# Normalised tokens made feature-major by VectorE and DRAM, with the norm weights in the matrices

## The chip, the cores and the metric

The kernel runs on one core of a Trainium2 chip. Five engines work beside each other: TensorE (PE; its weight loads are listed apart as PEld), VectorE (DVE), ScalarE (ACT), GpSimd (POOL) and SyncE (SP, which here only issues DMAs). The metric is the time of one execution in microseconds on the device. Three executions of the kernel before gave 1006.23, 1006.74 and 1008.61 us; their median, 1006.74 us, is the time before.

## What is computed

Sixteen elements of 256 tokens with 256 features, each with a context of 77 tokens, go through a decoder layer (self attention, cross attention, a gated MLP, each behind an RMS norm), and then through a second block of cross attention, a narrow MLP and self attention with layer norms. Everything is in 32-bit floats. The part that the change touches:

```python
def rmsnorm(x, w, eps=EPS):
    var = jnp.mean(jnp.square(x), axis=-1, keepdims=True)
    return x * jax.lax.rsqrt(var + eps) * w
...
h = rmsnorm(hidden_states, sa_norm_w)
h = residual + attention(h, h, sa_wq, sa_wk, sa_wv, sa_wo)
hn = rmsnorm(h, ca_norm_w)
h = residual + attention(hn, context, ca_wq, ca_wk, ca_wv, ca_wo)
hn = rmsnorm(h, mlp_norm_w)
h = residual + silu(hn @ w_gate) * (hn @ w_up) @ w_down
```

Attention has 16 heads of 16 features. `rmsnorm`'s result is used only as the left side of products with `sa_wq`, `sa_wk`, `sa_wv`, `ca_wq`, `w_gate` and `w_up`.

## The kernel before

Tokens lie on partitions: an element `b` is a tile of 128 partitions x 2 token tiles x 256 features (`h`), loaded by pairs of elements. A product needs its inputs with features on partitions, so that each norm is followed by a transposition.

For each element and each of the three norms (`sa`, `ca`, `mlp`), `rmsnorm` (lines 339 to 354) runs two squares with a sum on ScalarE (L347), a scale on VectorE and a power on GpSimd (`rsqrt`, L195 and L197), and two scalings on ScalarE that write `hn` (L353). `weighted_T` (lines 356 to 366) then transposes `hn` by four 128x128 TensorE transposes (`transposed`, L205) into a PSUM bank, and two ScalarE activations (L365) bring it to SBUF as `hnT`, each with the norm's weights as a scale for each partition. `project_T` (L423) multiplies `hnT` with a matrix: `psq` and `psk` in `self_operands`, `pscq` in `cross_queries`; `psv` (L672) takes `hnT` as the stationary side. In `mlp`, `pg` and `pu` (L752) are gate and up, `wd` (L782) is down. There is one buffer for each of `hnT_sa`, `hnT_ca` and `hnT_mlp`, and three for `hn`.

Attention: `sc` (L498) makes self scores, from which VectorE takes maxima (`nmax`, L503); `st` (L559) makes them again, transposed and with the maxima in, for the exponentials on ScalarE (`pT`, L567); `po` (L601) multiplies with the values. `csc`, `cst` and `cpo` are the same for the cross attention. All of `sc`, `st`, `csc` and `cst` write one tile of four PSUM banks (`ps_sc`), of which there is one. `wo` and `cwo` (L640) are the output projections; VectorE adds them to `h` (L645). Some 32x32 block transposes on VectorE turn attention outputs (L611, L631).

The order of the work is made by a planner written in the kernel (`Order`): each stage of each element is a stream of steps with engines, durations, needs, and buffers that it takes and gives back. The planner keeps a clock for each engine and at each turn takes the step with the best rank among those that can start, where `RANKS` gives each kind of stage a rank. A step of TensorE has a tile shape, full, row or column (`f`, `r`, `c`), with a price for a turn between shapes. `lag` is a time after a step's end until what it gives is there. Instructions are then issued engine by engine in that order, which the engines follow.

SP issues the loads of tokens and contexts, most constants, and the stores of the output. ScalarE issues four matrix loads at the start, GpSimd one. Eight completion counters are shared in turn by the DMAs of SP and ScalarE, so that a DMA's issue waits until the DMA that had its counter eight DMAs earlier has landed.

Of the kernel before, what the change touches and what calls it, by code (L numbers as in the profile page):

```python
# [15 lines left out]
P = 128  # L16
D = 256
# [12 lines left out]
def kernel(  # L30
# [24 lines left out]
    pool = ctx.enter_context(tc.tile_pool(name="work", bufs=2))  # L55
    small = ctx.enter_context(tc.tile_pool(name="small", bufs=2))
    ps_sc = ctx.enter_context(tc.tile_pool(name="ps_sc", bufs=1, space=PSUM))
    ps_po = ctx.enter_context(tc.tile_pool(name="ps_po", bufs=1, space=PSUM))
# [18 lines left out]
    def tokens(ap, u):  # L77
# [3 lines left out]
    BUFS = {  # L81
        "h": 4, "cx": 1, "cx2": 2, "hn": 3, "hnT_sa": 1, "hnT_ca": 1, "hnT_mlp": 1, "ctxT": 1,
        "qx": 3, "kx": 3, "vone": 3, "cqT": 1, "cqx": 1, "ckm": 1, "ckx": 1, "cvone": 2, "pT": 3,
# [25 lines left out]

    def load_matrix(src, name, eng):  # L110
        rows, cols = src.shape
        t = const.tile([P, rows // P, cols], F32, tag=name, name=name)
        eng.dma_start(t, src.rearrange("(c p) n -> p c n", p=P))
        return t

    def load_columns(src, name, eng):
        t = const.tile([P, NC], F32, tag=name, name=name)
        eng.dma_start(t, src.rearrange("(c p) -> p c", p=P))
        return t
# [11 lines left out]
    make_identity(nc, ident)  # L131
    sa_nw = load_columns(sa_norm_w, "sa_nw", nc.gpsimd)

    vones, cvones, maxes = [], [], ([], [])
    for i in range(3):
        t = const.tile([P, QT, NH, 2 * HD], F32, tag=f"vone{i}", name=f"vone{i}")
        nc.vector.memset(t, 1.0)
        vones.append(t)
    wq = load_matrix(sa_wq, "wq", nc.scalar)
    wk = load_matrix(sa_wk, "wk", nc.scalar)  # L140
    wv = load_matrix(sa_wv, "wv", nc.scalar)
    wo = load_matrix(sa_wo, "wo", nc.scalar)
    load_tokens(1)
    ca_nw = load_columns(ca_norm_w, "ca_nw", nc.sync)
    cwk = load_matrix(ca_wk, "cwk", nc.sync)
    cwv = load_matrix(ca_wv, "cwv", nc.sync)
    cwq = load_matrix(ca_wq, "cwq", nc.sync)
    cwo = load_matrix(ca_wo, "cwo", nc.sync)
    mlp_nw = load_columns(mlp_norm_w, "mlp_nw", nc.sync)
    wg = load_matrix(w_gate, "wg", nc.sync)  # L150
    wu = load_matrix(w_up, "wu", nc.sync)
    wd = load_matrix(w_down, "wd", nc.sync)
# [67 lines left out]

    STANDS_BACK = {"rf": 2, "cf": 2, "fc": 10}

# [16 lines left out]
    class Order:  # L239
# [35 lines left out]
        def put(self, st, t):  # L275
# [27 lines left out]
            for k in s.rel:  # L303
                self.freed[k[0]][self.held.pop(k)] = done
            for k in s.gives:
# [6 lines left out]
        def run(self):  # L312
            while self.streams:
                best = None
                aux = []
                for st in self.streams:
                    t = self.start(st)
                    if t is None:
                        continue
                    if st.step.pe:  # L320
                        turn, wait = self.shape + st.step.shape, t - self.clock["P"]
                        late = wait > 100
                        rank = st.rank[0] + STANDS_BACK.get(turn, 0) + 0.05 * wait
                        key = (late, t if late else 0, rank, st.rank[1])
                        if best is None or key < best[0]:
                            best = (key, st, t)
                    else:
                        e = st.step.ops[0][0]
                        aux.append((max(t + T_NEXT, self.clock[e]), st.rank, st, t))
                if aux:  # L330
                    b, _, st, t = min(aux, key=lambda a: a[:2])
                    if best is None or b + sum(o[1] for o in st.step.ops) <= best[2] + best[1].step.pe + 800:
                        self.put(st, t)
                        continue
                assert best, [(st.rank, vars(st.step)) for st in self.streams]
                self.put(best[1], best[2])


    def rmsnorm(b, kind, needs):
# [12 lines left out]
        for t in range(QT):  # L352
            nc.scalar.activation(hn[:, t, :], h[:, t, :], AF.Copy, scale=r[:, t : t + 1])  # L353
        return hn

    def weighted_T(hn, b, w, kind):

        yield Step(
            4 * T_TR, ops=[("A", 470)] * NC, acq=[(f"hnT_{kind}", b)],
            rel=[("hn", f"{kind}{b}")], gives=[(f"hnT_{kind}", b)],  # L360
        )
        tp = transposed(hn, f"{kind}{b}")
        dst = pool.tile([P, NC, S], F32, tag=f"hnT_{kind}", name=f"hnT_{kind}{b}", bufs=1)
        for c in range(NC):
            nc.scalar.activation(dst[:, c], tp[:, c], AF.Copy, scale=w[:, c : c + 1])  # L365
        return dst

# [45 lines left out]

    def project_T(w, srcT, name, steps=None):

        n = srcT.shape[-1]
        for m in range(NC):
            if steps:
                yield next(steps)
            if m == 0:  # L420
                ps = mm_bank(name)
            for c in range(NC):
                nc.tensor.matmul(  # L423
                    ps[:, m * n : (m + 1) * n], lhsT=w[:, c, m * P : (m + 1) * P],
                    rhs=srcT[:, c, :], start=(c == 0), stop=(c == NC - 1),
                )
        return ps[:, : NC * n].rearrange("p (m n) -> p m n", m=NC)
# [219 lines left out]
    def self_operands(a):  # L647
        b = a.b
        hn = yield from rmsnorm(b, "sa", [("x", b // UB)])
        hnT = yield from weighted_T(hn, b, sa_nw, "sa")  # L650
        ps = yield from project_T(wq, hnT, f"psq{b}", in_halves(
            ops=[("A", 690)] * 2, needs=["wq"], acq=[("qx", b)], gives=[a.key("q")]
        ))
        a.qx = a.tile("qx", [P, NC, 2, S])
        masked(a.qx[:, :, 0], a.qx[:, :, 1], ps)
        ps = yield from project_T(wk, hnT, f"psk{b}", in_halves(
            ops=[("V", 545)] * 4, needs=["wk"], acq=[("kx", b)], gives=[a.key("k")],
# [9 lines left out]
        for t in range(QT):  # L667
# [3 lines left out]
            for c in range(NC):  # L671
                nc.tensor.matmul(  # L672
                    ps[:, t * D : (t + 1) * D], lhsT=hnT[:, c, t * P : (t + 1) * P],
                    rhs=wv[:, c, :], start=(c == 0), stop=(c == NC - 1),
# [4 lines left out]
    def cross_keys(pair):  # L679
# [6 lines left out]
        for c in range(NC):  # L686
            for i in range(UB):
# [7 lines left out]
                   acq=[("ckm", u), ("ckx", u)], gives=[t.key("k") for t in pair])  # L695
        ps = yield from project_T(cwk, ctxT, f"psck{u}")
        km = a.tile("km", [P, NC, 2, UB * SK])
# [18 lines left out]
    def cross_queries(a):  # L716
        b = a.b
        hn = yield from rmsnorm(b, "ca", [("h", b)])
        hnT = yield from weighted_T(hn, b, ca_nw, "ca")
        ps = yield from project_T(cwq, hnT, f"pscq{b}", in_halves(  # L720
            ops=[("A", 585), ("A", 690), ("A", 690)], needs=["cwq"],
            acq=[("cqT", b), ("cqx", b)], rel=[("hnT_ca", b)], gives=[a.key("q")],
# [8 lines left out]
    def mlp(b):  # L731
        hn = yield from rmsnorm(b, "mlp", [("ch", b)])
        hnT = yield from weighted_T(hn, b, mlp_nw, "mlp")
        for f in range(0, NF, 2):
            banks = []
            for w, n in ((wg, "pg"), (wu, "pu")):
                if n == "pg":
                    steps = in_halves(
                        ops=[("A", 600), ("V", 690, 1)], needs=["wg"],
                        acq=[("sg", b, f)] + [("gT", b)] * (f == 0), free=f > 0,  # L740
# [6 lines left out]
                for i in range(2):  # L747
# [3 lines left out]
                    for c in range(NC):  # L751
                        nc.tensor.matmul(  # L752
                            ps[:, i * S : (i + 1) * S],
                            lhsT=w[:, c, (f + i) * P : (f + i + 1) * P], rhs=hnT[:, c, :],
                            start=(c == 0), stop=(c == NC - 1),
# [363 lines left out]
    def loads():  # L1119
        for u in range(NU):  # L1120
            yield Step(ops=[("S", 100)], acq=[("h", u)], gives=[("x", u)] * (u > 1), lag=5000)
            if u > 1:
                load_tokens(u)

    def context_loads():
        for u in range(NU):
# [6 lines left out]
    def second_loads():  # L1133
# [5 lines left out]
    order.done.update({  # L1139
        ("x", 0): 5e3, ("x", 1): 20e3, "wq": 8e3, "wk": 9e3, "wv": 10e3, "cwk": 12e3,  # L1140
        "cwv": 13e3, "cwq": 14e3, "wg": 18e3, "wu": 21e3, "wd": 24e3, "late": 14e3, "small": 28e3,
    })
# [4 lines left out]
        "second_constants": (1, 50, 0),  # L1147
        "outputs": (4.5, -1, 50),
        "exponentials": (-2.5, -50, 4),
        "projection": (1.5, -50, 1.5),  # L1150
        "cross_outputs": (3, 0, 50.25),
        "cross_exponentials": (-100, 0, 0),
        "cross_projection": (-50, 0, 0),
        "self_maxima": (0, -50, -100),
        "cross_maxima": (-49, 0, 0),
        "cross_queries": (0, 1, -49.5),
        "self_operands": (-1.5, 0, -0.5),
        "cross_keys": (2, 0, 0),
        "mlp": (4.75, -0.25, -3.5),
        "second_context": (6, 0, -50),  # L1160
        "second": (3, 0, -50),
# [6 lines left out]

    add("loads", 0, 0, loads())
    add("loads", 0, 1, context_loads())  # L1170
    add("loads", 0, 2, second_loads())
# [17 lines left out]
    for u in range(NU):  # L1189
# [6 lines left out]
        mybir.EngineType.PE, mybir.EngineType.Activation, mybir.EngineType.DVE,  # L1196
        mybir.EngineType.Pool,
    }
# [33 lines left out]
```

## Time and profile before

One profiled execution took 1005.27 us, of which the span from its first to its last instruction is 1003.3 us.

| | us | share of span |
|---|---|---|
| profiled execution | 1005.27 | |
| its span | 1003.3 | |
| TensorE busy | 965.4 | 96% |
| VectorE busy | 589.6 | 59% |
| ScalarE busy | 504.4 | 50% |
| GpSimd busy | 81.4 | 8% |
| data moved by DMA | 17.57 MB | |

How to read it. The page lists busy time by engine; divides the span in 40 equal slices with a digit for each engine (tenths of the slice that it was busy; 9 is 90% or more), and for the TensorE clock that was granted; names the chain of work that ended last; and groups instructions by source line, tile, shape and count, with busy time, mean duration in ns, the idle time of the engine before them and what ended it. Matmuls are pipelined, so that the duration of one is longer than the time from its start to the next one's. A 32-bit matmul is two instructions. The window sums give for each stretch of time its length, the busy us of PE, PEld, DVE, ACT and POOL (with instruction counts), the granted clock as a share, the DMAs' share and GB/s.

In the chain that ended last TensorE has 85% of the span, VectorE 7%, ScalarE 4%, DMA 2%.

### The profile page before, as it was taken

How to read it: one execution, taken by the hardware profiler on the slowest of the kernel's cores; microseconds unless marked ns; L12 is line 12 of the kernel's file. 1: busy time of each engine (PE TensorE's matmuls, PEld its weight loads, DVE VectorE, ACT ScalarE, POOL GpSimd, SP SyncE). 2: the span in 40 equal slices, each digit the busy share in tenths (PEclk: the TensorE clock that was granted, in tenths of full speed). 3: DMA queues.
4: the chain of work that ended last, by engine and by line, in shares of the span. 5: the costliest groups of instructions: out<-in, count | busy, mean ns of one | idle time of the engine just before them, and what ended most of it. 6: DMA issues, size and time to landing. Idle time of an engine off the chain costs nothing.

```text
span 1003.3 us, 18784 instructions
## 1 busy us (share of the span) xinstructions
PE 965.4 (96%) x8106; PEld 711.2 (71%) x8106; DVE 589.6 (59%) x1025; ACT 504.4 (50%) x854; POOL 81.4 (8%) x119
## 2 busy tenths in 40 slices
PE   6888899999999999999999999999999999999995
PEld 5656567777776877768777777777777677787772
DVE  3765456568666457474765567645775445545452
ACT  4545545452743745535573626457257538433532
POOL 2100000000100101000110001001001002000210
PEclk9999699999999999999999999999999999999995
DMA  9100000000000000010000100010000000000000
GB/s 304 30 2 7 1 1 1 8 2 1 1 8 19 26 8 1 8 43 2 8 1 8 44 7 1 8 43 1 7 2 2 22 8 2 1 22 1 1 22 22
DMA packets 17347, 17.57 MB, mean 18 GB/s; under 512 B 2832, under 2 KB 16752, under 8 KB 17264
## 3 DMA queue, kind: packets, MB, share of 16 engines
q1 hardware_dynamic: 16144, 15.32, 4.8%
q8 instruction: 64, 1.05, 0.4%
q10 hardware_dynamic: 1088, 1.05, 0.3%
q14 instruction: 19, 0.16, 0.1%
q0 software_dynamic: 32, 0.00, 0.0%
HBM read 12.13 MB, written 4.19 MB: 16 GB/s over the span
## 4 chain that ended last, share of the span: by engine, by line
PE 85%; DVE 7%; ACT 4%; DMA 2%; issue 1%; POOL 0%; POOLq 0%; ACTq 0%; DVEq 0%
PE wd L782 12%; PE pg L752 10%; PE pu L752 10%; PE sc L498 6%; PE st L559 6%; PE po L601 5%; PE pscq L423 3%; PE cst L559 3%; PE psq L423 3%; PE psk L423 2%; PE cpo L601 2%; PE psv L672 2%; DVE nmax L503 2%; ACT pT L567 2%; PE csc L524 2%; PE cwo L640 2%
## 5 line engine op out<-in xcount | busy, mean ns | idle before, releaser
L503 DVE TENSOR_REDUCE nmax<-sc 128x8 f32<-128x2048 f32 x64 | 146.3, 2286 | 35.5 <-PE sc L498 34.6
L567 ACT ACTIVATE pT<-st 128x2048 f32<-128x2048 f32 x64 | 120.1, 1876 | 77.4 <-PE st L559 76.9
L752 PE MATMUL pg<-hnT_mlp,wg 128*128 128x256 f32 x512 | 131.3, 390 | 0.0
L752 PE MATMUL pu<-hnT_mlp,wu 128*128 128x256 f32 x512 | 128.5, 385 | 0.0
L782 PE MATMUL wd<-wd,gT 128*128 128x256 f32 x512 | 126.1, 388 | 0.0
L752 PEld LDWEIGHTS pg<-hnT_mlp,wg 128*128 128x128 f32 x512 | 93.5, 192 | 23.3 <-issue 11.9
L782 PEld LDWEIGHTS wd<-wd,gT 128*128 128x128 f32 x512 | 92.4, 190 | 21.6 <-issue 10.0
L752 PEld LDWEIGHTS pu<-hnT_mlp,wu 128*128 128x128 f32 x512 | 93.8, 190 | 18.4 <-issue 6.9
L567 ACT ACTIVATE cpT<-cst 77x2048 f32<-77x2048 f32 x32 | 59.9, 1873 | 60.0 <-PE cst L559 60.0
L763 DVE SCALAR_TENSOR_TENSOR sg<-sg,pg 128x512 f32<-128x512 f32 x64 | 43.9, 686 | 75.2 <-ACT sg L762 74.9
L762 ACT ACTIVATE sg<-pg 128x512 f32<-128x512 f32 x64 | 38.1, 595 | 82.2 <-PE pg L752 82.0
L764 DVE SCALAR_TENSOR_TENSOR gT<-sg,pu 128x512 f32<-128x512 f32 x64 | 43.8, 684 | 34.3 <-PE pu L752 33.1
L601 PE MATMUL po<-pT,vone 128*32 128x256 f32 x1024 | 62.6, 382 | 0.0
L531 DVE TENSOR_REDUCE nmax<-csc 128x16 f32<-128x1232 f32 x32 | 46.1, 1441 | 18.2 <-PE csc L524 18.0
L197 POOL TENSOR_TENSOR rstd_n<-ve_n,neg_half 128x4 f32<-128x4 f32 (+3 forms) x28 | 23.2, 829 | 332.7 <-DVE ve_n L195 313.0
L601 PEld LDWEIGHTS po<-pT,vone 128*32 128x32 f32 x1024 | 29.9, 110 | 23.9 <-issue 7.7
L787 DVE TENSOR_TENSOR h<-h,wd 128x256 f32<-128x256 f32 x32 | 13.4, 417 | 51.6 <-PE wd L782 51.4
L423 PE MATMUL psq<-hnT_sa,wq 128*128 128x256 f32 x128 | 34.1, 406 | 0.6 <-ACT hnT_sa L365 0.6
L423 PE MATMUL psk<-hnT_sa,wk 128*128 128x256 f32 x128 | 33.0, 396 | 0.0
L601 PE MATMUL cpo<-cpT,cvone 77*32 77x256 f32 x512 | 32.9, 397 | 0.0
L423 PE MATMUL pscq<-hnT_ca,cwq 128*128 128x256 f32 x128 | 32.7, 401 | 0.1
L672 PE MATMUL psv<-wv,hnT_sa 128*128 128x256 f32 x128 | 31.9, 388 | 0.0
(603 smaller groups left out, 1550.7 us busy)
## 6 DMA issues: line engine op xcount, KB each, us to landing
h<-in_x_dram SPq DMA_DIRECT2D x7, 512.0 KB
out_dram<-h SPq DMA_DIRECT2D x7, 512.0 KB
cx<-in_ctx_dram SPq DMA_DIRECT2D x16, 154.0 KB
wg<-in_L_xattn_w_gate_dram SPq DMA_DIRECT2D x1, 1024.0 KB
wu<-in_L_xattn_w_up_dram SPq DMA_DIRECT2D x1, 1024.0 KB
wd<-in_L_xattn_w_down_dram SPq DMA_DIRECT2D x1, 1024.0 KB
h<-in_x_dram SPq DMA_DIRECT2D x4, 128.0 KB
out_dram<-h SPq DMA_DIRECT2D x2, 256.0 KB
```

Of the source, the lines that this page charges most:

```text
L423: nc.tensor.matmul(ps[:, m * n : (m + 1) * n], lhsT=w[:, c, m * P : (m + 1) * P], rhs=srcT[:, c, :], start=(c == 0), stop=(c == NC - 1),)
L498: nc.tensor.matmul(sc[:, j, (1 - e) * S : (2 - e) * S], lhsT=a.qx[rg, c, e, qt * P : (qt + 1) * P], rhs=a.kx[rg, c, e], start=True, stop=True,
L503: nc.vector.tensor_reduce(maxima_of(nm, qt)[:, :, c::NC], sc.rearrange("p j (y k) -> p j y k", y=2), AX.X, ALU.max, negate=True,)
L531: nc.vector.tensor_reduce(maxima_of(nm, qt), sc[:, :, : 2 * NC * SK].rearrange("p j (n k) -> p j n k", k=SK), AX.X, ALU.max, negate=True,)
L559: nc.tensor.matmul(st[:nk, j, e * S : (e + 1) * S], lhsT=a.kx[rg, c, e, kc * P : kc * P + nk], rhs=a.qx[rg, c, e], start=True, stop=True,)
L567: nc.scalar.activation(a.pT[k][:nk].rearrange("p j e q -> p j (e q)"), st[:nk], AF.Exp, scale=HD ** -0.5,)
L601: nc.tensor.matmul(po[RG * j : RG * (j + 1), e, :], lhsT=a.v[:nk, kc, 8 * c + 2 * j + e, :], rhs=pT[:nk, j, e, :], start=(kc == 0 and e == ...
L672: nc.tensor.matmul(ps[:, t * D : (t + 1) * D], lhsT=hnT[:, c, t * P : (t + 1) * P], rhs=wv[:, c, :], start=(c == 0), stop=(c == NC - 1),)
L752: nc.tensor.matmul(ps[:, i * S : (i + 1) * S], lhsT=w[:, c, (f + i) * P : (f + i + 1) * P], rhs=hnT[:, c, :], start=(c == 0), stop=(c == N ...
L763: nc.vector.scalar_tensor_tensor(sg, sg, 1.0, ps, ALU.add, ALU.mult)
L764: nc.vector.scalar_tensor_tensor(gT[:, f : f + 2, :].rearrange("p f q -> p (f q)"), sg, 0.5, banks[1], ALU.mult, ALU.mult,)
L782: nc.tensor.matmul(ps[:, :D], lhsT=gT[:, f, i * P : (i + 1) * P], rhs=wd[:, f, :], start=(f == 0), stop=(f == NF - 1),)
```

## The change

For elements 2 to 15 the TensorE transposes and their evictions are replaced. VectorE transposes `hn` in blocks of 32x32 into a tile `hb` (one buffer); SP writes `hb` to a tile in DRAM and reads it back in another order of rows into `hnT`, which brings the blocks to their partitions. Elements 0 and 1 keep the TensorE transposes; their `hn` is written with features permuted and `hnT` is copied without weights.

The features come out in another order on the partitions, r before j where feature is 32j + r. So the six matrices that meet `hnT` are loaded in that order, by two DMAs each (`spread`), and so are the norm weights. `weights()` multiplies the norm weights into the matrices once, `wq`, `wk`, `wv` and `cwq` on VectorE, `wg` and `wu` on GpSimd. Tokens lie in `hnT` in an order a, i, t; `tokens_moving` reads them in natural order as a moving operand, `tokens_still` in stored order for keys and values. In the `sa` tiles the two feature chunks alternate, so that a chunk is read at a step of two elements (8 bytes); in the `ca` and `mlp` tiles a chunk lies in runs of 32 elements.

Besides, `hn` has two buffers in place of three, the planner's ranks and three of its constants are changed, a released buffer counts from the end of the `lag`, and SP's instructions are issued in the planner's order too.

```diff
-        "h": 4, "cx": 1, "cx2": 2, "hn": 3, "hnT_sa": 1, "hnT_ca": 1, "hnT_mlp": 1, "ctxT": 1,
+        "h": 4, "cx": 1, "cx2": 2, "hn": 2, "hb": 1, "hnT_sa": 1, "hnT_ca": 1, "hnT_mlp": 1, "ctxT": 1,
...
-    def load_matrix(src, name, eng):
+    def load_matrix(src, name, eng, spread=False):
...
+        if spread:
+            for c in range(NC):
+                eng.dma_start(
+                    t[:, c], src[c * P : (c + 1) * P].rearrange("(j r) n -> r j n", r=RG)
+                )
+        else:
+            eng.dma_start(t, src.rearrange("(c p) n -> p c n", p=P))
...
-    STANDS_BACK = {"rf": 2, "cf": 2, "fc": 10}
+    STANDS_BACK = {"rf": 5, "cf": 5, "fc": 10}
...
-                self.freed[k[0]][self.held.pop(k)] = done
+                self.freed[k[0]][self.held.pop(k)] = done + s.lag
...
-                        key = (late, t if late else 0, rank, st.rank[1])
+                        key = (late, t + T_TURN[turn] if late else 0, rank, st.rank[1])
...
-                    if best is None or b + sum(o[1] for o in st.step.ops) <= best[2] + best[1].step.pe + 800:
+                    if best is None or b + sum(o[1] for o in st.step.ops) <= best[2] + best[1].step.pe + 500:
...
-    def weighted_T(hn, b, w, kind):
-
+    def tokens_moving(t, c):
+
+        return t[:, :, :, c].rearrange("p a i t -> p i a t")
+
+    def tokens_still(t, c):
+
+        return t[:, :, :, c].rearrange("p a i t -> p (a i t)")
+
+    def feature_major(hn, b, kind):
...
+        shape = [P, P // RG, QT] + ([RG, NC] if by_tokens else [NC, RG])
+        if b < UB:
...
+            tp = transposed(hn, name)
+            dst = pool.tile(shape, F32, tag=key, name=f"hnT_{name}", bufs=1)
+            for c in range(NC):
+                nc.scalar.copy(
+                    tokens_moving(chunks(dst), c),
+                    tp[:, c].rearrange("p (i a t) -> p i a t", i=QT, t=RG),
+                )
+            return chunks(dst)
+
+        yield Step(ops=[("V", 690)], acq=[("hb", name)], rel=[("hn", name)])
+        hb = pool.tile(shape, F32, tag="hb", name=f"hb_{name}", bufs=BUFS["hb"])
+        nc.vector.transpose(
+            chunks(hb), hn.rearrange("p i (c j r) -> p j i c r", c=NC, r=RG),
+        )
+        yield Step(ops=[("S", 600)], rel=[("hb", name)], gives=[("blocks", name)], lag=2000)
+        blocks = dram.tile([P, P // RG, QT * NC * RG], F32, tag="blocks", name=f"blocks_{name}")
+        nc.sync.dma_start(blocks, hb.rearrange("p j i t c -> p j (i t c)"))
         yield Step(
-            4 * T_TR, ops=[("A", 470)] * NC, acq=[(f"hnT_{kind}", b)],
-            rel=[("hn", f"{kind}{b}")], gives=[(f"hnT_{kind}", b)],
-        )
-        tp = transposed(hn, f"{kind}{b}")
-        dst = pool.tile([P, NC, S], F32, tag=f"hnT_{kind}", name=f"hnT_{kind}{b}", bufs=1)
-        for c in range(NC):
-            nc.scalar.activation(dst[:, c], tp[:, c], AF.Copy, scale=w[:, c : c + 1])
-        return dst
+            ops=[("S", 600)], needs=[("blocks", name)], acq=[(key, b)], gives=[(key, b)], lag=2000
+        )
+        dst = pool.tile(shape, F32, tag=key, name=f"hnT_{name}", bufs=1)
+        nc.sync.dma_start(
+            dst.rearrange("p a i t c -> p a (i t c)"),
+            blocks.rearrange("(a r) j x -> (r j) a x", r=RG),
+        )
+        return chunks(dst)
...
+    def weights():
+
+        for name, w, nw, eng, ns in (
+            ("wq", wq, sa_nw, "V", 200), ("wk", wk, sa_nw, "V", 200), ("wv", wv, sa_nw, "V", 200),
+            ("cwq", cwq, ca_nw, "V", 200), ("wg", wg, mlp_nw, "G", 1000), ("wu", wu, mlp_nw, "G", 1000),
+        ):
+            yield Step(ops=[(eng, ns)] * NC, needs=[name + " in"], gives=[name], free=True)
+            for c in range(NC):
+                (nc.vector if eng == "V" else nc.gpsimd).tensor_scalar(
+                    w[:, c], w[:, c], nw[:, c : c + 1], None, ALU.mult
+                )
...
-        "outputs": (4.5, -1, 50),
-        "exponentials": (-2.5, -50, 4),
-        "projection": (1.5, -50, 1.5),
-        "cross_outputs": (3, 0, 50.25),
+        "outputs": (6.5, -1, 50),
+        "exponentials": (-52.5, -50, 4),
+        "projection": (-0.5, -50, -0.5),
+        "cross_outputs": (5, 0, 0.25),
...
-        "self_maxima": (0, -50, -100),
+        "self_maxima": (-0.25, -50, -100),
...
-        "cross_queries": (0, 1, -49.5),
-        "self_operands": (-1.5, 0, -0.5),
-        "cross_keys": (2, 0, 0),
-        "mlp": (4.75, -0.25, -3.5),
-        "second_context": (6, 0, -50),
+        "cross_queries": (-2, 1, -49.5),
+        "self_operands": (-2, 0, -0.5),
+        "cross_keys": (1.75, 0, 0),
+        "mlp": (4.25, 2.75, -2.5),
+        "second_context": (5.5, 0, -50),
```

## The prediction

> **What bounds the kernel now.** First the page's busy shares, then the slices, then the window sums by stage, then the time order of TensorE in one stage.
>
> ```profile
> PE 965.4 (96%) x8106; PEld 711.2 (71%) x8106; DVE 589.6 (59%) x1025; ACT 504.4 (50%) x854; POOL 81.4 (8%) x119
> PE   6888899999999999999999999999999999999995
> PEclk9999699999999999999999999999999999999995
> ```
>
> ```profile
> 20.00:125.00 105.00, 91.06 (x834) 61.32 (x834) 65.76 (x99) 56.17 (x103) 8.00 (x21) 0.92 0.10 24
> 125.00:930.00 805.00, 804.32 (x6908) 597.25 (x6907) 485.90 (x808) 414.44 (x687) 57.95 (x69) 1.00 0.03 10
> 930.00:974.60 44.60, 43.61 (x265) 35.67 (x263) 22.59 (x68) 17.43 (x33) 7.51 (x9) 1.00 0.04 12
> 974.60:1003.30 28.70, 14.95 (x67) 7.90 (x66) 9.82 (x36) 8.32 (x14) 2.71 (x4) 0.58 0.06 19
> ```
>
> Columns are length, then busy us of PE, PEld, DVE, ACT and POOL, the granted clock, and DMA. From 125 to 930 us TensorE is busy 804.3 of 805 us at full clock, VectorE 60%, ScalarE 51%: there the kernel is a queue of matmuls, and a TensorE instruction removed is time removed. From 20 to 125 us TensorE idles 14 us and runs at 0.92: the one four-bank score tile sets the pace. The last 28.7 us, after the last down projection, are a serial chain of small steps.
>
> A busy TensorE is not one at its peak, so I take start-to-start times:
>
> ```profile
> 518.33 0.66 PE L205 MATMUL tp_ca<-ident,hn_ca 128*128 128x128 f32 x4
> 518.82 1.03 PE L752 MATMUL pu<-hnT_mlp,wu 128*128 128x256 f32 x4
> ...
> 536.50 0.60 PE L205 MATMUL tp_mlp<-ident,hn_mlp 128*128 128x128 f32 x4
> 536.94 1.03 PE L782 MATMUL wd<-wd,gT 128*128 128x256 f32 x4
> ```
>
> Four transposes hold TensorE 0.49 us behind a score step and 0.44 us between plain matmuls.
>
> **What goes.** The built program has 168 TensorE transposes fewer: 42 tiles (14 elements, three norms), four each; elements 0 and 1 keep theirs. 42 x 0.44 is 18.5 us, 42 x 0.49 is 20.6; I take 19.5, 0.465 each. In the order, 13 rows of transposes stand ahead of the first gate matmul before and 9 after, so 4 tiles lie in the start, where TensorE isn't the bound: 38 x 0.465 = **-17.7 us**.
>
> [...] transposes overlap and one follows another after 0.11 us. The mean in the row below (288 ns: 48 us) misleads in the same way.
>
> ```profile
> L205 PE MATMUL tp_mlp<-ident,hn_mlp 128*128 128x128 f32 x64 | 10.6, 288 | 0.2 <-ACT hn_mlp L353 0.2
> L365 ACT ACTIVATE hnT_mlp<-tp_mlp,mlp_nw 128x256 f32<-128x256 f32 x32 | 13.4, 470 | 26.8 <-PE tp_mlp L205 26.7
> ```
>
> ScalarE loses 84 evictions of 0.47 us, 39.5 us. It is 51% busy and not the bound: nothing on the path.
>
> **What comes.** VectorE gets 42 block transposes. Nearest row:
>
> ```profile
> L631 DVE STREAM_TRANSPOSE oT__1339<-oq__1289 x1: 704/704/704, 156.4 to 156.4; 128x512 f32<-128x512 f32 x1
> ```
>
> 42 x 0.70 = 29.4 us; VectorE goes from 60% to 64% in the long stage and TensorE's queue hides it. The new output steps 8 bytes in the self tiles, which no row shows: 0.64 (the shortest such row) to 1.4 us (twice), 27 to 59 us, still below 70%. Without that cover each would add 0.7 us to its own chain.
>
> SP gets 84 DMAs, 256 KB out and 256 KB back for each tile. Nearest rows, in the chain of waits:
>
> ```profile
> 323.81 2.96 DMA out_dram<-h
> ...
> 326.78 3.43 DMA h<-in_x_dram
> ```
>
> Both move 512 KB. Half the bytes cost 1.5 to 3.0 us out and 1.7 to 3.4 back. The read has as many runs as the load of h (512, of 512 bytes), so I put it near the top, 3.0; the write has 128 rows of 2 KB, 2.5. Round trip 5.5, ends 3.2 and 6.4. The planner allows 600 + 2000 ns each way, 5.2. From the tile numbers I counted the TensorE work that stands between each read's place and its first matmul. In 30 of 42 it is over 4 us, for the MLP mostly 10 to 40. In ten (7 of `pscq`, 3 of `psq`) it is 2.6 to 3.7, against 2.6 allowed. Two have less: tile 2 in the start (1.3), and the last `pscq`, whose read falls inside a down projection that the count can't split, 0 to 2.6: TensorE waits there by plan, 0 to 2.6 us, I take 1. A round trip 0.3 late costs about 1 us more over these 12; one 1.2 late (the upper end) 8; an early one nothing.
>
> SP issues in order. A read waits for its own write, and the next write stands behind it; the single `hb` then holds VectorE, and behind that transpose the evictions for TensorE. Four times an output store and a load of h that waits for it (10.0 us in all, longest 2.5) stand in front of a handoff; three times it is an MLP read with 29 us or more to spare, once the `ca` write of a tile with 2.8: up to 2.5 us, I take 1. **Waits: 1 + 1 + 1 = +3 us.**
>
> Start. Eight matrix scalings come to VectorE (128x256; the nearest row, L382, takes 0.41), 3.3 us. Six fill its idle time before the first `kx` (it waits 5.2 us there); the two for `cwq` stand between the first and the second score maximum, on the chain: 0 to 0.8, I take 0.5. Four 128x1024 on POOL (2.4 us each by L966, which has two inputs, at most 9.5) end long before the gate matmul at 124 us. Halved loads make 7 DMA issues on ScalarE ahead of its first table load in place of 4, each about 0.5; but `wo` waited for the landing of `wq` until 4.3 us anyway, and now for a smaller piece: -0.3 to +1.5, I take +0.5. The permuted copies of elements 0 and 1 keep count and size: 0, at most 0.5 each.
>
> The ranks change the start too. Ahead of the first gate matmul stand, before, 12 `sc`, 10 `st`, 4 `csc`, 2 `cst`; after, 12, 12, 3, 2. A score tile turns over in 3.9 (`sc`), 3.15 (`st`), 2.6 (`csc`) and 3.1 us (`cst`) in the start's timeline, so the first gate comes 2 x 3.15 - 2.6 = 3.7 us later, with 2.6 us more useful matmul work done: +1.1. TensorE's turns between full, row and column tiles hardly change (198 to 204, 178 to 177, 42 to 46, 18 to 12): 0. The order from the last down projection on is the same: 0.
>
> Operands. `psq` and `psk` (256 instructions, 216 ns start to start, 55 us) now read at a step of 8 bytes, `pscq`, gate and up in runs of 32. No row shows a strided moving operand, so the bounds are far apart: 0 to double, +55 us. [...] I take 0. No run here shows it yet. Loading `hnT_sa` as weights for `psv` hides behind 216 ns matmuls now (190).
>
> **Sum.** -17.7 + 3 + 0.5 + 0.5 + 1.1 = -12.6 us. The profiled execution took 1005.27 (span 1003.3 and 2.0 around it): 992.7. The median of the runs is 1.5 above it: **994 us**.
>
> **The rivals.**
> *The start gets better*: the dip of the clock (slice 5, 0.6; some 8 us lost between 102 and 127) goes[...]. For it: the ranks move much there. Against: the score tile still sets the pace. 994 - 8 and no waits: 983, down to 977.
> *The gain is eaten in the start*: the tiles of elements 2 and 3, which now take 5.5 us more, delay the score chain. By the chain, tile 2 is back at about 39 us, just ahead of the second score step of element 1 at 41, so the cover is thin. Three such misses of 3 us, 9 us: 1003.
> *The round trip decides* (slower). Place: `pscq` and `psq` behind their reads, with SP in order. Each us of lateness beyond 0.5 costs about 11 us over the 12 tight tiles. The gain is gone from 1.7 us late, a round trip near 7; at 2.5 late it is 25 us, 1019. For it: so many thin margins. Against: 512 KB took 6.4 in all.
> *The stride costs* (slower too): from 25% more on `psq` and `psk` on; at half, 27 us, 1021.
> That the change doesn't do what it says is excluded for the transposes by the built order.
>
> **How the numbers follow.** Forecast 0.58 (own range 986 to 1001), better start 0.13, eaten 0.14, round trip 0.09, stride 0.06. A change below 0.3% (3 us) can't be told from none. Faster: 0.58 + 0.13 + half of "eaten" = 0.78; same 0.07; slower 0.15. The range leaves out the slower pair and the best corner: 978 to 1006.
>
> **What would show it.** Right: from about 125 us on TensorE still over 99% busy, with `psq` and `pscq` hardly waiting for a DMA, `psq` matmuls at 380 ns and 216 start to start, VectorE near 64%, the round trip 5 to 6 us, the first gate at 125 to 130 us. Wrong: long waits of `pscq` for `hnT_ca`, longer `psq` and `psk` matmuls, idle TensorE at 30 to 60 us, another dip of the clock.

## The result, and the profile after

Twelve runs of the changed kernel have a median of 1001.06 us (999.98 to 1004.80), twelve of the kernel before beside them 1006.19. The ratio is 0.9955 (95% interval 0.9941 to 0.9969). That is 5.1 us less by the medians and 4.5 by the ratio: a gain, where the sum gave 12.6. The profiled execution took 1001.62 us, its span is 999.8.

The page's busy shares and slices after (clock in tenths):

```profile
PE 951.9 (95%) x7938; PEld 691.2 (69%) x7938; DVE 621.1 (62%) x1075; ACT 475.8 (48%) x770; POOL 93.7 (9%) x124
PE   5879799999999999999999999999999999999995
PEclk9899799999999999999999999999999999999995
```

The 168 transposes are gone (8106 matmul records, 7938 after), and ScalarE is 28.6 us less busy, where 39.5 had been counted. Slices 1, 3 and 5 are lower than before and slice 4 is higher; the clock dips in slices 2 and 5, where it dipped in slice 5 alone. The window sums after, in the columns of the prediction:

```profile
20.00:125.00 105.00, 88.90 (x787) 59.55 (x785) 66.02 (x102) 51.07 (x88) 18.91 (x24) 0.90 0.19 54
125.00:930.00 805.00, 797.95 (x6811) 582.72 (x6810) 516.40 (x851) 394.03 (x625) 61.20 (x71) 1.00 0.10 34
```

From 125 to 930 us TensorE now idles 7 us, where it idled 0.7. VectorE is at 516.4 of 805 us, 64%. What TensorE waits for in that stretch (us in all, times, longest):

```profile
PE wo L699 <- DVE oT__3932 L690: 1.6, 1, 1.6
PE cwo L699 <- DVE ve_n L208: 1.2, 1, 1.2
PE st L618 <- ACT pT L626: 1.0, 1, 1.0
...
PE pscq L482 <- DMA hnT_ca<-blocks_ca: 0.6, 2, 0.4
```

The wait that the prediction feared, `pscq` for its blocks, is 0.6 us. A single `wo` waits longer, for an attention output of VectorE. The chain of waits says why (start, duration):

```profile
464.42 1.23 DVE h L1174
...
465.72 2.91 DMA out_dram<-h
...
468.64 4.64 DMA h<-in_x_dram
...
473.31 0.52 ACT sq_sa L360 x2
...
475.44 0.92 ACT hn_sa L370 x2
...
476.38 0.73 DVE hb_sa L412
...
478.09 0.72 DVE oT__3932 L690
...
478.95 1.10 PE wo L699 x4
```

A pair of elements is finished, stored, and the next pair is loaded into the same buffer: 7.6 us from the last addition until ScalarE can square. ScalarE and VectorE are held in order behind the load: `hb_sa` waits for `hn_sa`, and `oT`, which has nothing to do with either, stands behind `hb_sa` on VectorE.

To add this up I price each TensorE step by its undisturbed start-to-start time (0.816 us for 16 score matmuls, 0.216 for a plain one, and so on) and call the rest **loss** (good to about 1 us, since the prices can be chosen a little differently). The steps sum to 924.9 us before and 906.8 after, 18.1 less. The loss grows from 78.3 to 93.0: by 7.8 up to 140 us, by 8.8 from 140 to 930 us (16.6 to 25.4), and it falls by 1.9 behind that.

### The profile page after: what moved, and what is told of

It reads as the page before. It is cut to its first block, busy times and chain, and to the rows that moved or that the text cites. A ratio compares the mean times of both kernels' runs of the same rounds, so it can differ in the third digit from the quotient of the medians.

```text
span 999.8 us, 18578 instructions
## 1 busy us (share of the span) xinstructions
PE 951.9 (95%) x7938; PEld 691.2 (69%) x7938; DVE 621.1 (62%) x1075; ACT 475.8 (48%) x770; POOL 93.7 (9%) x124
## 4 chain that ended last, share of the span: by engine, by line
PE 84%; DVE 6%; DMA 4%; ACT 4%; issue 1%; POOL 0%; POOLq 0%; SPq 0%; ACTq 0%; DVEq 0%
PE pg L811 11%; PE pu L811 11%; PE wd L841 10%; PE st L618 7%; PE sc L557 6%; PE po L660 4%; PE psq L482 3%; PE wo L699 3%; PE pscq L482 3%; PE cpo L660 3%; PE cst L618 3%; PE cwo L699 3%; PE psk L482 3%; PE psv L731 2%; PE csc L583 2%; DMA h<-in_x_dram 2%
## 5 line engine op out<-in xcount | busy, mean ns | idle before, releaser
L811 PE MATMUL pg<-hnT_mlp,wg 128*128 128x256 f32 x512 | 129.8, 387 | 0.0
L823 DVE SCALAR_TENSOR_TENSOR gT<-sg,pu 128x512 f32<-128x512 f32 x64 | 43.7, 683 | 29.3 <-PE pu L811 28.1
L660 PEld LDWEIGHTS po<-pT,vone 128*32 128x32 f32 x1024 | 29.7, 109 | 27.1 <-issue 9.3
L210 POOL TENSOR_TENSOR rstd_ca<-ve_ca,neg_half 128x2 f32<-128x2 f32 x16 | 11.1, 697 | 304.3 <-DVE ve_ca L208 304.2
```

What stands on the lines that cost most here:

```text
L660: nc.tensor.matmul(po[RG * j : RG * (j + 1), e, :], lhsT=a.v[:nk, kc, 8 * c + 2 * j + e, :], rhs=pT[:nk, j, e, :], start=(kc == 0 and e == ...
L811: nc.tensor.matmul(ps[:, i * S : (i + 1) * S], lhsT=w[:, c, (f + i) * P : (f + i + 1) * P], rhs=tokens_moving(hnT, c), start=(c == 0), sto ...
L823: nc.vector.scalar_tensor_tensor(gT[:, f : f + 2, :].rearrange("p f q -> p (f q)"), sg, 0.5, banks[1], ALU.mult, ALU.mult,)
```

## The experiments

All were timed beside the kernel before, whose median was 1004.6 to 1006.2 us from batch to batch. The numbers behind each time are its ratio to that and the 95% interval. Runs of different batches are compared by these ratios; 0.001 is 1 us.

**The way and the ranks taken apart.** First the changed kernel with TensorE transposes everywhere, and the kernel before with the new ranks.

```diff
-            if b < UB:
+            if True:
...
-        if b < UB:
+        if True:
```

> The changed kernel with the TensorE transposes for all elements (weights in the matrices, spread loads, ranks and constants stay). Theory A (the handoff through DRAM costs some 9 us of waits between 140 and 930 us): TensorE gets its 18 us of transposes back, the waits go; about 1010 us, the loss of TensorE from 140 to 930 us back near 17. Rival B (the new ranks and constants cost it, not the handoff): the loss stays near 25 and the time is near 1019. In both the first psq stays near 13.5 us.

> The kernel before with the ranks and the three planner constants of the change and nothing else. Theory A (ranks cost only in the start, through two more st steps ahead of the first gate): the first gate 3 to 5 us later than 123.8, the loss from 140 to 930 us within 2 us of before; 1007 to 1010 us. Rival B (the ranks cost the long stretch too): 1014 us or more. Rival C (the ranks are a gain by themselves): under 1004.

Measured: 1045.31 us (1.0396, 1.0379 to 1.0413) and 1044.66 us (1.0387, 1.0367 to 1.0406). The first lies outside both of its theories. The second is "the ranks cost the long stretch too", which allowed any time from 1014 on; nothing foresaw 38 us. A third run left the trip through DRAM out and let the planner know it:

```diff
-        yield Step(ops=[("V", 690)], acq=[("hb", name)], rel=[("hn", name)])
+        yield Step(ops=[("V", 690)], acq=[(key, b)], rel=[("hn", name)], gives=[(key, b)])
...
-            chunks(hb), hn.rearrange("p i (c j r) -> p j i c r", c=NC, r=RG),
+            chunks(dst), hn.rearrange("p i (c j r) -> p j i c r", c=NC, r=RG),
```

> The changed kernel in which VectorE transposes straight into hnT and nothing goes through DRAM; the blocks then stay on their partitions, so that the products get other features than the reference's. Theory A (the handoff's lateness costs some 9 us from 140 to 930 us and some in the start): 990 to 993 us, the loss from 140 to 930 us near 17. Rival B (ranks, or the transposes on VectorE, cost it): 998 to 1001 us, the loss stays near 25.

Measured: 1027.12 us (1.0213, 1.0197 to 1.0228), 26 us slower with less to do. In all three the ranks belong to another set of steps than the one that is planned, and the order that comes out is worse: 26 us over the changed kernel without the trip, 38 and 39 over the kernel before with TensorE transposes. The loss from 140 to 930 us is 46 to 48 us in each. (The third also has VectorE wait until the single `hnT` buffer is free, so that its 26 us need not be the order's alone.) These runs say nothing of the parts; they say that a part can be judged only in an order that is held. From here on, unless it is said otherwise, the planner counts what it counted before and only the issued instructions change.

**The transposes alone.** In the kernel before, `hnT` is filled from `hn` itself.

```diff
-        tp = transposed(hn, f"{kind}{b}")
+        tp = transposed(hn, f"{kind}{b}") if b < UB else hn
```

> The kernel before, order held, without the TensorE transposes of elements 2 to 15: ScalarE fills hnT from hn itself, so that the products get untransposed tokens. Nothing comes in their place. It measures the term of the prediction alone: 38 x 0.465 = 17.7 us less, 988 to 989. If the transposes were partly hidden, or other waits close the gap, less: 992 or more.

Measured: 999.55 us (0.9941, 0.9927 to 0.9954) against 1005.24. The 18.5 us of TensorE work bring 5.7. The chain of waits of this run at the largest new stall:

```profile
322.95 4.93 DMA out_dram<-h
...
327.90 3.80 DMA h<-in_x_dram
...
331.78 0.52 ACT sq_sa L347 x2
...
333.62 1.77 ACT pT L567
...
335.44 2.09 PE st L559 x16
```

The same store and load: ScalarE sits 3.8 us in front of `sq_sa`, an exponential (`pT`) stands behind it, and `st` for the next scores waits 2.8 us for that. The kernel before has the same pair of DMAs here, 2.96 and 3.43 us in the prediction's rows, and ScalarE waited 1.4 us for it without TensorE noticing. Of the 2.4 us that it waits longer here, 0.9 come from ScalarE's earlier arrival. The other 1.5 are the DMAs': they are issued 0.9 us earlier and land 1.5 us later. This store is the one slow one of four; for two of the other reloads ScalarE waits 1.8 and 1.9 us, in place of 1.4 and 1.5. Behind the stall the granted clock is at half for 3.4 us (the last number but two):

```profile
335.30:338.70 3.40, 3.26 (x19) 2.28 (x20) 0.69 (x1) 2.47 (x5) 0.00 (x0) 0.50 0.00 0
```

The 16 `st` take 2.09 us there, and 1.15 at full clock. By an estimate (half of 3.4) that is another 1.7 us. The kernel before has full clock in this place.

**The reload of h.** The stores ahead of the four reloads left out, in the changed kernel and in the bare one.

```diff
-        nc.sync.dma_start(tokens(out, u)[:, first * QT : first * QT + NT], h)
+        if u > 3:
+            nc.sync.dma_start(tokens(out, u)[:, first * QT : first * QT + NT], h)
```

> The changed kernel, order held, without the output stores of the first four pairs, so that each of the four reloads of h that follow a store starts some 2.9 us earlier. Theory C (the store and reload of h, 7.6 us in a row, which TensorE's shorter work no longer covers, holds ScalarE and VectorE in order and in the end TensorE): the stall of 1.6 us ahead of wo at 475 us goes, and those near 590 and 725 shrink; the loss from 140 to 930 us falls by 3 to 6 us, time 995 to 998. Rival (the waits elsewhere take its place): 1000 to 1001.

> The kernel before, order held, without the TensorE transposes of elements 2 to 15 (as in the run of 999.55) and without the output stores of the first four pairs. Theory C: the stall of 2.8 us for st at 335 us and its follower of 1.1 us go, 4 to 6 us less: 994 to 996. Rival (ScalarE's or VectorE's other work is what st waits for): 999 to 1000.

Measured: 997.80 us (0.9933, 0.9920 to 0.9946), 2.2 below the changed kernel by the ratios, with intervals that overlap a little; and 993.85 us (0.9889, 0.9876 to 0.9902), 5.2 below the bare one, clear of the noise. In the changed kernel without those stores TensorE is idle for 3.7 us from 125 to 930 us, where it was 7.0:

```profile
125.00:930.00 805.00, 801.28 (x6836) 586.54 (x6836) 518.58 (x858) 395.41 (x628) 61.14 (x71) 1.00 0.10 31
```

So the reload is worth 2.2 us there by the times and 3.3 by the trace. TensorE's waits that are left:

```profile
PE st L618 <- ACT pT L626: 1.0, 1, 1.0
PE cst L618 <- ACT cpT L626: 0.7, 1, 0.7
PE st L618 <- DVE nmax L590: 0.7, 1, 0.7
PE pu L811 <- DVE sg L822: 0.5, 1, 0.5
PE pscq L482 <- DMA hnT_ca<-blocks_ca: 0.2, 1, 0.2
```

`wo` and `cwo` are gone from the list. The bare kernel without stores also lets the saved work be read row by row against the kernel before: where four transposes stood, the steps around them close up by 0.436 us between plain matmuls and by 0.49 behind a score step. One tile of 38 closes up by nothing. The 38 tiles behind 125 us sum to 17.2 us. Between those places, from 140 to 930 us, the kernel gives back 4.5 us, in pieces of under 0.3 us each. Of these, 16 pieces of 0.10 us, 1.6 in all, stand right behind a removed tile. One such place, in the kernel before:

```profile
220.73 0.66 PE L205 MATMUL tp_ca<-ident,hn_ca 128*128 128x128 f32 x4
221.22 1.89 PE L752 MATMUL pu<-hnT_mlp,wu 128*128 128x256 f32 x8
```

and in the bare one without stores:

```profile
220.21 1.15 PE L559 MATMUL st<-qx__822,kx__844 32*128 32x256 f32 x16
221.29 1.99 PE L752 MATMUL pu<-hnT_mlp,wu 128*128 128x256 f32 x8
```

The same eight `pu` take 1.99 us in place of 1.89. This is the turn from row to full tiles: where a plain step follows a score step directly, its second matmul starts 0.320 us behind its first (59 places in the kernel before), and 0.219 behind transposes. The transposes had taken that turn on themselves. What the other 2.9 us are is open.

Then a form that keeps the stores: two halves, one element each, so that the first half's load waits for the first half's store only.

```diff
-        nc.sync.dma_start(tokens(out, u)[:, first * QT : first * QT + NT], h)
+        for i in range(first * QT, first * QT + NT, QT):
+            nc.sync.dma_start(tokens(out, u)[:, i : i + QT], hs[u][:, i : i + QT])
...
+        if u >= BUFS["h"]:
+            parts = [slice(0, QT), slice(QT, NT)]
+        for part in parts:
+            nc.sync.dma_start(hs[u][:, part], tokens(x, u)[:, part])
```

> The changed kernel, order held, with output stores and the last four reloads of h in two halves each (one element each), so that the first half's reload starts when the first half's store is done. Theory C: the first element's h is there 1.5 to 2.5 us earlier, 1 to 3 us less: 998 to 1000. Rival (more DMAs in SP's queue cost as much as they bring): 1001 or more.

> The kernel before, order held, with output stores and the last four reloads of h in halves. Theory C (the reload became the limit only when TensorE's work ahead of it got shorter; before, no instruction of ScalarE waits for it for long): no change, 1004 to 1006. Rival (faster reloads help any version): 1003 or less.

Measured: 997.95 us (0.9930, 0.9917 to 0.9944) on the changed kernel, 2.5 less by the ratios; on the kernel before 1004.39 against 1004.75 (0.9995, 0.9987 to 1.0003), nothing. The reloads that ScalarE waits for now take 5.0 to 5.1 us from the first store to the square, where the chain above has 7.6. The planner counts 5.1 for it in both kernels. So the faster reload brought something only where TensorE had less work. In the bare kernel that is the missing transposes alone, since the order is the same; in the changed kernel the order is new too, and which of the two uncovers the reload isn't separated.

**The trip through DRAM.** Left out, with the order held (`blocks` and its two DMAs gone, `dst` in four rotating tiles), and then the read doubled.

```diff
-        nc.sync.dma_start(
-            dst.rearrange("p a i t c -> p a (i t c)"),
-            blocks.rearrange("(a r) j x -> (r j) a x", r=RG),
-        )
+        for _ in range(2):
+            nc.sync.dma_start(
+                dst.rearrange("p a i t c -> p a (i t c)"),
+                blocks.rearrange("(a r) j x -> (r j) a x", r=RG),
+            )
```

> The changed kernel with its order of work held, step for step, and the trip through DRAM left out: VectorE transposes straight into hnT (four rotating tiles, the memory of before), so that blocks stay on their partitions and the products get other features than the reference's. The planner still counts the trip. Theory A (what the trip really takes on the chip, beyond the plan, costs it): TensorE's loss from 140 to 930 us falls from 25 to 17 or less, time 989 to 993 us. Rival (the loss is the order's own, planned in): the loss stays above 22, time 998 to 1001.

> The changed kernel, order held, in which each read of the blocks is issued twice, so that each handoff is later by one read (3.5 to 4.4 us) and SP is held that much longer. Theory A with the prediction's price (11 us per us of lateness over the 12 tight tiles): 30 to 45 us more, 1030 to 1045. Rival (one late tile delays the chain once and later slack takes it up): under 15 us more, below 1016.

Measured: 1001.20 us without the trip (0.9960, 0.9948 to 0.9973), the same as with it; 1043.21 us with two reads (1.0376, 1.0362 to 1.0390), 42 more. TensorE's waits with two reads:

```profile
PE pscq L483 <- DMA hnT_ca<-blocks_ca: 22.4, 12, 3.0
PE psq L483 <- DMA hnT_sa<-blocks_sa: 4.4, 2, 2.4
```

Twelve waits of `pscq` and two of `psq`, where the changed kernel has two of 0.6 us in all. Over the whole span the waits for these reads are 30.4 us. The clock stands at half for 44 us until the last down projection, against 20 in the changed kernel; behind 140 us it falls five times, within 1.4 us of the end of such a wait (2.0 to 2.4 us), and stays down for 3.4. Since the reload could have hidden a cost of the trip, the trip was left out once more beside the halves:

> The changed kernel, order held, with halves and without the trip through DRAM (VectorE transposes straight into hnT, other features). If the reload's stall hid a cost of the trip: 2 to 3 us below the halves alone, 995 to 996. If the trip is covered: as the halves alone, 997 to 999.

Measured: 997.04 us (0.9922, 0.9907 to 0.9938), 0.8 below the halves alone by the ratios, with intervals that overlap and alone would allow up to some 3 us. By TensorE's waits for the blocks the trip costs 0.6 us.

**The start.** `wv` and `wo` issued by GpSimd, alone and with the halves; and plain matrices.

```diff
-    wv = load_matrix(sa_wv, "wv", nc.scalar, True)
-    wo = load_matrix(sa_wo, "wo", nc.scalar)
+    wv = load_matrix(sa_wv, "wv", nc.gpsimd, True)
+    wo = load_matrix(sa_wo, "wo", nc.gpsimd)
```

> The changed kernel with the loads of wv and wo issued by GpSimd in place of ScalarE, so that no DMA issue that waits for a counter stands ahead of ScalarE's first table load. Theory A (that queue is what delays the start): table load at about 3.4 us in place of 7.3, the first psq at 10 to 11 us in place of 13.5, the first score at 19 to 20, the time 1.5 to 3 us shorter: 998 to 999.5. Rival (the score tile's pace or the matrix scalings absorb it): the first psq moves, the first gate and the time don't: 1001.

> The halves of the run beside it, and the loads of wv and wo issued by GpSimd. If both gains add: 996 to 999. If the clock's dips in the start decide: as the run beside it.

> The changed kernel, order held, with the matrices and norm weights loaded by one DMA each as before and the scalings of the matrices left out (so that the products take other features and no norm weights). Theory (these carry the loss of the start beyond the plan): first psq at 10.6 instead of 13.5, first gate 3 to 4 us earlier, time 3 to 4 us shorter, 997 to 998. Rival (the order of VectorE's own work in the start carries it): the first gate at 130 or later, 999.5 to 1001.

The time order of ScalarE in the changed kernel:

```profile
3.63 2.99 ACTq L116 DMA_DIRECT2D wv<-in_L_xattn_sa_wv_dram  x2
6.67 0.61 ACTq L120 DMA_DIRECT2D wo<-in_L_xattn_sa_wo_dram  x1
7.31 1.28 ACT L360 ACT_TABLE_LOAD   x1 [7.31 <-DMA wv<-in_L_xattn_sa_wv_dram]
```

and with the two loads on GpSimd's queue:

```profile
3.36 1.28 ACT L360 ACT_TABLE_LOAD   x1 [3.36 <-issue]
```

Halved loads use up the eight counters: the second half of `wv` waits for one and is issued at 6.09 us, `wo` behind it at 6.67 (in the kernel before, `wo` alone of ScalarE's four loads waited, until `wq`, which had its counter, had landed at 4.28), and the table load, at 4.71 us before, comes at 7.31. Moved, it comes at 3.36, the first `psq` at 10.48 us in place of 13.46 and the first gate at 130.3 in place of 132.9. The time did not follow: 1000.92 us (0.9955, 0.9937 to 0.9972), the changed kernel's ratio; its six executions lie between 998.0 and 1003.5. With halves it is 995.63 us (0.9900, 0.9886 to 0.9914), 3.0 below the halves alone by the ratios, so what this queue is worth lies between 0 and 3 us and isn't settled. Plain matrices give 998.54 us (0.9932, 0.9919 to 0.9944), 2.3 less by the ratios, with the first `psq` at 10.50 and the first gate at 129.8.

Two signs of being wrong that the prediction named for the start are there. One window in the changed kernel, and the same in the kernel before:

```profile
30.00:40.00 10.00, 6.80 (x65) 4.60 (x63) 9.63 (x14) 1.82 (x6) 9.15 (x5) 0.85 0.25 74
```

```profile
30.00:40.00 10.00, 9.46 (x77) 7.29 (x70) 8.19 (x9) 4.72 (x12) 2.41 (x12) 1.00 0.08 19
```

TensorE idles 3.2 us there, while VectorE is busy for 9.6 of 10, and the clock is at 0.85, where it was at full. From 20 to 125 us it is 0.90 in place of 0.92, about 2 us (an estimate: 0.02 of 105).

**The step of the moving operand.** In the records of the changed kernel `psq` and `psk` start 226 ns apart, `pscq`, gate and up 216, and all of them 216 before.

```diff
-        ps = yield from project_T(wq, lambda c: tokens_moving(hnT, c), S, f"psq{b}", in_halves(
+        ps = yield from project_T(wq, lambda c: plain(hnT, c), S, f"psq{b}", in_halves(
```

`psk` likewise; `plain` takes 256 neighbouring elements.

> The kernel with halves and with wv and wo on GpSimd's queue (995.63), order held, in which psq and psk read 256 neighbouring elements of hnT in place of every second one (so that they take tokens and features in another order). If the 8-byte step is what holds them: 216 ns start to start in place of 226, and 256 x 10 ns = 2.6 us less at most, 993 to 994.5. If it is something else: 226 ns and 995 to 996.5.

The durations of `psq`'s matmuls (min, median, max in ns), in the changed kernel and in this run:

```profile
L482 PE MATMUL psq<-hnT_sa,wq x128: 385/387/793, 13.5 to 758.4; 128*128 128x256 f32 x128
```

```profile
L493 PE MATMUL psq<-hnT_sa,wq x128: 378/379/794, 10.8 to 751.4; 128*128 128x256 f32 x128
```

379 ns is also the duration that this matmul had before, within 1 ns, and the starts are 216 ns apart again. The time is 994.58 us (0.9899, 0.9882 to 0.9916) against 995.63 (0.9900): the step shows in the starts and not in the ratios. 256 x 10 ns allow 2.6 us at most.

**Ranks fitted again.** The kernel with halves and the moved queue, the turn's price in the planner nearer to the trace, with and without truer lags for the trip, and ranks fitted anew to the planner's clock.

```diff
-        "ff": 0, "fr": 93, "fc": 93, "rf": 364, "cf": 366, "rc": 260, "cr": 261, "rr": 0, "cc": 0,
+        "ff": 0, "fr": 93, "fc": 93, "rf": 300, "cf": 366, "rc": 260, "cr": 261, "rr": 0, "cc": 0,
...
-        yield Step(ops=[("S", 600)], rel=[("hb", name)], gives=[("blocks", name)], lag=2000)
+        yield Step(ops=[("S", 600)], rel=[("hb", name)], gives=[("blocks", name)], lag=1500)
...
-            ops=[("S", 600)], needs=[("blocks", name)], acq=[(key, b)], gives=[(key, b)], lag=2000
+            ops=[("S", 600)], needs=[("blocks", name)], acq=[(key, b)], gives=[(key, b)], lag=3400
...
-        "cross_outputs": (5, 0, 0.25),
+        "cross_outputs": (3, 51, 2.25),
...
-        "cross_queries": (-2, 1, -49.5),
+        "cross_queries": (0, 1, -49.5),
```

> Halves, wv and wo on GpSimd's queue, and the planner's prices nearer to the trace (turn from row to full tiles 300 ns in place of 364, the write's lag 1.5 us, the read's 3.4 us), with ranks fitted anew to the planner's own clock. If the small waits come from wrong prices: 985 to 992. If the planner's clock, [...] is no better a guide than before: 994 to 1000.

> As the kernel beside it, with only the turn's price corrected (300 ns) and the lags of the trip left at 2.0 us each, ranks fitted anew. If the trip's price matters for the order: worse than the kernel beside it, with waits of pscq for its read; if not, the two are within 3 us.

Measured: 1002.38 us (0.9968, 0.9957 to 0.9979) and 1002.45 us (0.9966, 0.9953 to 0.9979), both worse than the 995.63 that they started from. `psq` and `pscq` do wait more for their reads in the second (2.9 us, against 1.4), as it should be, but it decides nothing. The loss from 140 to 930 us is 29.3 and 27.7 us, against 22.1. My fit was a miss: what the planner's clock gains isn't what the chip gains.

The version that does the same work and is fastest is the changed kernel with halves and the two loads on GpSimd: 995.63 us (0.9900).

## Why the prediction missed

**What goes (-17.7): the step from TensorE's time to the kernel's time failed.** The sentence that failed is "there the kernel is a queue of matmuls, and a TensorE instruction removed is time removed". With nothing put in their place, 18.5 us of removed work brought 5.7 us. "804.3 of 805" says that TensorE waited for nothing while the order fitted. It doesn't say how far the next limit is. That limit was the reload of h, whose 6.4 us the prediction had in its own rows and priced only as a delay of the handoff behind it. It holds 5.2 us of the bare kernel, with one slow store and a spell of half clock in that, and 2.2 to 3.3 of the changed one. The 4.5 us of small pieces that the bare kernel gives back had no term either. The size at the tiles was right: 17.2 us by start-to-start times. But 1.6 us of that were turns from row to full tiles, which "hardly change: 0" left out: they didn't go with the transposes.

**Waits (+3): about nothing.** The trip takes 5.9 and 6.4 us in the changed kernel's chain of waits (2.0 for the write), and with two reads the write and the first of them take 4.6 to 5.9: 5.5 was a fair guess. Leaving the trip out brings 0 to 0.8 us. The third rival's price came out near, in part by luck. One more read, 2.7 to 3.8 us, cost 42 us, 11 to 16 for each us against its 11. But twelve `pscq` and two `psq` wait behind 125 us, where the count of tight tiles had 8 and 3, and part of the 42 is the clock, which the price didn't have. So the kernel stands close to an edge that it doesn't touch.

**Start (+0.5, +0.5, +1.1): too small.** Up to 140 us the loss grows by 7.8. Forecast were 2.1, and 1.9 for the four tiles that were not counted as saved. The matrices cost 2.3 us, not 1.0. "`wo` waited for the landing of `wq` until 4.3 us anyway, and now for a smaller piece" was wrong: with seven issues it is `wv` that waits for counters, until 6.1 us. The first gate came at 132.9 us, not 125 to 130. What of the rest of the start is the ranks' doing could not be separated, since ranks can't be changed alone.

**Operands (0): wrong.** The 8-byte step costs 10 ns of 216 (`psq` and `psk`: 226 in the changed kernel, 216 with neighbouring elements), at most 2.6 us over the kernel. The 0 was the author's estimate, with no row behind it. For `pscq`, gate and up, in runs of 32, it held: 216 before and after.

**What held.** 0.70 us for each transpose of VectorE (median 0.705 for `hb_ca`), VectorE at 64%, and the tail: 29.7 us from the last down projection's tile to the end before, 29.2 after. Of the rivals, "the gain is eaten in the start" named about the right size, 1003, and the start did lose. But its reason, score steps missed for late tiles, is not what the runs showed: without the trip the first gate still comes at 133.3 us.

Put together: -17.2, +2.2 to 3.3 for the reload, +4.5 for small pieces, +2.3 for the matrices, 0 to 2.6 for the step and 0 to 0.8 for the trip give -8.2 to -3.7; measured is -5.1. The 4.5 are read from the bare kernel and not measured in the changed one. There the loss from 140 to 930 us grew by 8.8; the reload (3.3) and the step (168 instructions there, 1.7) leave 3.8 for them. That the ranks cost 1.1 in the start, as predicted, or something else, is inside this scatter and open.

## What to carry to other kernels

A TensorE that is 99.9% busy is a bound only as far as the second limit lets it (18.5 us removed brought 5.7 here): before counting removed work as time, look in the trace for chains that the removed work covers, a store and reload into the same buffer above all, and ask what stands in order behind the instruction that waits for them. Ask too which turn the removed step had taken on itself. Test it by removing the work and putting nothing in its place, in the same order. Where a planner's ranks are fitted to one set of steps, a part taken out or put back measures the planner (26 to 39 us here), unless the order is held.

## What was not expected of the hardware

A 128x256 matmul whose 32-bit moving operand steps by 8 bytes (`psq` and `psk` in the changed kernel) started its successor after 226 ns in place of 216.

In the bare run and in the one with two reads TensorE's clock fell to half at waits of only 2.0 to 2.8 us, for 3.4 us at a time behind 140 us. It didn't at each of them: a wait of 3.0 us had no such spell.

While GpSimd scaled `wu`, a 5x256 scaling on VectorE took three times as long as in the kernel before. GpSimd and VectorE in the changed kernel, then VectorE before:

```profile
33.23 5.67 POOL L1192 TENSOR_SCALAR wu<-wu,mlp_nw 128x1024 f32<-128x1024 f32 x2
38.19 1.10 DVE L895 TENSOR_SCALAR scratch<-scratch,f5m 5x256 f32<-5x256 f32 x1
```

```profile
43.92 0.34 DVE L836 TENSOR_SCALAR scratch<-scratch,f5m 5x256 f32<-5x256 f32 x1
```

It ends 0.39 us behind GpSimd. In the two runs with the moved queue it starts closer to GpSimd's end, takes 0.68 and 0.46 us, and again ends 0.39 to 0.40 us behind it; with plain matrices, where GpSimd scales nothing, it takes 0.33. Why it ends there is not shown. Reductions of VectorE beside GpSimd's scalings kept their 2.28 us.

A store of 512 KB took 2.91 us in the changed kernel's chain above and 4.93 in the bare one's, and the load of h behind it 4.64 and 3.80. In the first case the read of an MLP tile and two context loads were issued right behind the load of h; what slowed the store in the second is open.
